# Full-width f32 products for the first two chunks of a fused attention and expert kernel, with the weights' high and low parts made later

## The chip, the cores and the metric

The kernel runs on one core of one Trainium2 chip. The metric is the device time of one execution in microseconds, the median of several runs. The core has a matmul engine (TensorE, PE in the profile), VectorE (DVE), ScalarE (ACT), GpSimd (POOL) and SyncE (SP), which here issues all transfers.

## What is computed

The input x has 8 sequences of 1024 tokens with 256 features, in float32. In short form:

```
qkv = x @ Wqkv + b;  q, k, v = split(qkv)
q, k = q - mean(q), k - mean(k)            # over features
q2 = q*q / (sum(q*q) + eps), scaled to unit length over features
k2 = k*k / (sum(k*k) + eps), scaled to unit length over the 1024 tokens
t2 = q2 @ (k2^T @ v) / sqrt(1024)          # no softmax: linear attention
x  = layernorm(x + (v + t2) @ Wln + bln)
sel    = sigmoid(x @ expert_sel^T)         # 16 experts
scores = relu(x @ keys[e])                 # 128 hidden features each
out    = sum over e of sel[e] * (scores @ values[e])
x  = layernorm(x + out)
```

## The kernel before, in words

Work goes by chunks of 512 tokens, 16 in all, two to a sequence. The projections of v and of the output are folded: `wy` stands for identity plus Wv @ Wln less its mean, and a 256x256 matrix M per sequence (`mh`, `ml`) carries k2^T x through Wv and Wln. For one chunk there are these steps: `tokens_x` loads x transposed (`xf`), `tokens_n` loads x token by token (`nf`); `u_k` projects keys (`kp`), squares and normalizes them (`k`) and multiplies with x (`ap`); `u_m` makes M from the sums of both chunks of a sequence (`mc`, `pm`, `mt`); `u_q` projects queries (`qp`), normalizes and transposes them (`qt`); `u_y` adds x @ wy (`ymx`) and q2 @ M (`ymq`) in `yp` and makes the gates; `u_pair` runs the experts, with `h` for the first product and `w` for the second; `u_end` closes with the second layernorm.

Almost every product is made from split operands. A float32 tile is cast on ScalarE (or VectorE) to the reduced format fp32r, its high part, and VectorE or GpSimd subtracts that from the original for the low part. `passes3` (line 52) then makes three fp32r matmuls out of each product:

```python
    return [(ah, bh), (ah, bl), (al, bh)]
```

So x has `xh`, `xl` and `nh`, `nl`; the weights have `wkh`, `wkl` (lines 460 to 475), `wqh`, `wql` (line 1309) and `wyh`, `wyl` (1306 to 1308); normalized keys have `k2h`, `k2l` (594 to 596), queries `q2h`, `q2l` (758 to 760) and M has `mh`, `ml` (688 to 699). A few products use unsplit float32 tiles, among them the centring of the weights (`wq_c`, `wl_c`, line 482) and the spreading of the first gates (`gsp`, line 844). In the chunks 0 and 1 the key and query biases enter as one more matmul with `rows` and `bhl`; from chunk 2 on VectorE adds them.

The order of the work is not written by hand. Each step is a task with an engine (or a choice of two), a cost, a key and the buffers that it reads and writes (`Work.add`, line 116). `Work.order` (line 202) plays the tasks through with these costs, engine by engine, and the program is issued in that order. Tasks that lead to the second expert products of the first three experts of chunk 0 are the goals' forebears: `sharpen` ranks them by the path still ahead of them, and they go first. All others go by their key. Buffers come from pools with a fixed number of slots (lines 41 to 45), and a task can be chosen only when its slots are free: `ld2` with three slots takes staged loads, `xh`, `xl`, `s4`, `ych` and `ycl` take parts, `t2` takes short-lived tiles. While goals are outstanding and TensorE has nothing that is ready, the planner puts in two small matmuls (`keep_warm`, line 433; tile `warm`), planned at 0.44 us:

```python
                        if e == "T" and self.idle and issued and first and now > 0.4:
                            fill = Task()
```

On the chip these fills are ordinary instructions in TensorE's queue. At the start of the program (lines 1213 to 1225) stand the loads of `sk` (the key weights), of x for the chunks 0 and 1, and of the other weights; then `u_k(0)`, `u_k(1)`, `u_q(0)`, `u_m(0)`, the first expert weights and `u_y(0)` (1251 to 1319), and `steady` (1321) brings in the later chunks while the experts of earlier ones run.

Of the kernel before, what the change touches and what calls it, by code (L numbers as in the profile page):

```python
# [15 lines left out]
P = 128  # L16
D = 256
# [13 lines left out]
FAST_FROM = 1  # L31
FAST_AT = 0.39
# [69 lines left out]
class Work:  # L102
# [13 lines left out]
    def add(self, eng, cost, key, fn, r=(), w=(), port=False, after=()):  # L116
# [6 lines left out]
        for many, writes in ((r, False), (w, True)):  # L123
            for x in many:
                b, part = x if isinstance(x, tuple) else (x, None)
                for other, opart, owrites in b.accesses:
                    if (writes or owrites) and meet(part, opart) and other is not t:
                        t.deps.add(other)
                b.accesses.append((t, part, writes))
                t.bufs[b] = None  # L130
        for d in t.deps:
            d.outs.append(t)
# [190 lines left out]
def attn_ffn_kernel(ctx, tc, x, xT, wqT, wk, wvT, wlnT, bcols, brows, selT, keys, values, outT):  # L323
# [55 lines left out]
    def high(key, h, b, n, r, w, free=True):  # L379

        if free:
            add("VS", {"V": c_dve(n, fast=True), "S": c_act(n, plain=True)}, key,
                {"V": lambda: V.tensor_copy(h(), b()), "S": lambda: S.copy(h(), b())}, r=r, w=w, port={"V": True, "S": False})
        else:
            add("S", c_act(n, plain=True), key, lambda: S.copy(h(), b()), r=r, w=w)
# [74 lines left out]
    def centered_rows(key, b, h, l):  # L460
# [8 lines left out]
        for k in range(2):  # L469
            add("VS", {"V": c_dve(D, fast=True, ptr=True), "S": c_act(D)}, key, {  # L470
                "V": lambda k=k: V.tensor_scalar(h[:, k], b[:, k], m[:, k : k + 1], None, ALU.add),
                "S": lambda k=k: S.activation(h[:, k], b[:, k], AF.Identity, bias=m[:, k : k + 1]),
            }, r=[b, m], w=[(h, k)], port={"V": True, "S": False})
            add("V", c_dve(D, ptr=True), key, lambda k=k: V.scalar_tensor_tensor(
                l[:, k], b[:, k], m[:, k : k + 1], f(h[:, k]), ALU.add, ALU.subtract), r=[b, m, (h, k)], w=[(l, k)], port=True)
# [15 lines left out]
    def high_low(key, t, h, l):  # L491
        add("S", c_act(CH, plain=True), key, lambda: S.copy(h.ap, halves(t.ap)), r=[t], w=[h])
        add("V", c_dve(CH), key, lambda: V.tensor_tensor(l.ap, halves(t.ap), f(h.ap), ALU.subtract), r=[t, h], w=[l])
# [5 lines left out]
    def in_first(c, tag, other):  # L499
        return other if c == 1 else tag  # L500

    def tokens_x(c, key):
        xh[c], xl[c] = h, l = [sbuf(t, [P, 2, CH], f"{t}{c}", FR) for t in ("xh", "xl")]
        if c == 0:
            b = sbuf("g3", [P, 2, CH], f"xf{c}")
            for i in range(2):
                w = slice(i * CH // 2, (i + 1) * CH // 2)
                add("D", 1.05, key, lambda w=w: nc.sync.dma_start(out=b[:, :, w], in_=xTv[:, :, w]), w=[(b, i)])
            for i in range(2):
                w = slice(i * CH // 2, (i + 1) * CH // 2)  # L510
                high(key + 1.2, lambda w=w: h[:, :, w], lambda w=w: b[:, :, w], CH, [(b, i)], [(h, i)])
                apply(key + 1.5, lambda w=w: l[:, :, w], lambda w=w: b[:, :, w], lambda w=w: f(h[:, :, w]), ALU.subtract,
                      CH, [(b, i), (h, i)], [(l, i)])
            return
        split(c, key, "xf", lambda s: xTv[:, s, c * CH : (c + 1) * CH], h, l, CH)

    def split(c, key, name, src, h, l, width):

        rows = h.shape[1]
        n = 1 if c < 2 else 2  # L520
        for i in range(n):
            s = slice(i * rows // n, (i + 1) * rows // n)
            part = None if n == 1 else i
            b = sbuf("g3" if c < 2 else "ld2", [P, rows // n, width], f"{name}{c}_{i}")
# [865 lines left out]
```

## Time and profile before

| | |
|---|---|
| median of 3 runs | 1022.59 us (1020.59 to 1023.46) |
| the profiled execution | 1020.05 us |
| its span, first to last instruction | 1018.3 us |
| mean granted clock of TensorE | 0.996 |
| busy: PE, DVE, ACT, POOL | 1008.1, 784.8, 667.1, 470.5 us |
| DMA | 99.52 MB, mean 98 GB/s |
| first projection starts (`kp`) | 9.18 us |
| first product of queries and M (`yp<-q2h,mh`) starts | 42.48 us |
| first second-layer product of an expert (`w`) starts | 63.96 us |

A line of the profile's timeline has the start, the time of the whole group, the engine, the line of the program, the operation and the tiles as out<-in, the shape and the number of instructions. Matmuls are pipelined: the duration of one is longer than the step to the next, so costs of TensorE are read from start to start. A float32 product that is not split leaves two records, a split one leaves three.

### The profile page before, as it was taken

How to read it: one execution, taken by the hardware profiler on the slowest of the kernel's cores; microseconds unless marked ns; L12 is line 12 of the kernel's file. 1: busy time of each engine (PE TensorE's matmuls, PEld its weight loads, DVE VectorE, ACT ScalarE, POOL GpSimd, SP SyncE). 2: the span in 40 equal slices, each digit the busy share in tenths (PEclk: the TensorE clock that was granted, in tenths of full speed). 3: DMA queues.
4: the chain of work that ended last, by engine and by line, in shares of the span. 5: the costliest groups of instructions: out<-in, count | busy, mean ns of one | idle time of the engine just before them, and what ended most of it. 6: DMA issues, size and time to landing. Idle time of an engine off the chain costs nothing.

```text
span 1018.3 us, 16317 instructions
## 1 busy us (share of the span) xinstructions
PE 1008.1 (99%) x5757; PEld 874.3 (86%) x5757; DVE 784.8 (77%) x1363; ACT 667.1 (66%) x1497; POOL 470.5 (46%) x424
## 2 busy tenths in 40 slices
PE   9999999999999999999999999999999999999996
PEld 9978879888898988889888888988889888888885
DVE  7889888687776887768787687867878687686775
ACT  7767566675676757766676676757666675665543
POOL 1001585546564464655536574454654536233430
PEclk9999999999999999999999999999999999999999
DMA  6144323233232323323223231323323222223131
GB/s 202 44 135 125 116 94 125 93 90 101 82 121 68 115 94 104 93 89 103 93 89 108 87 115 63 115 94 103 105 71 109 93 85 83 83 85 104 64 125 42
DMA packets 65298, 99.52 MB, mean 98 GB/s; under 512 B 6336, under 2 KB 24896, under 8 KB 65216
## 3 DMA queue, kind: packets, MB, share of 16 engines
q1 hardware_dynamic: 65216, 98.48, 30.1%
q8 instruction: 45, 0.74, 0.3%
q14 instruction: 37, 0.30, 0.1%
HBM read 89.54 MB, written 8.91 MB: 97 GB/s over the span
## 4 chain that ended last, share of the span: by engine, by line
PE 93%; DVE 3%; POOL 2%; ACT 1%; DMA 1%; issue 1%; POOLq 0%; DVEq 0%; ACTq 0%; SPq 0%
PE w L1121 32%; PE h L358 17%; PE hx L1074 11%; PE yp L358 8%; PE qp L358 4%; PE hy L1074 4%; PE kp L358 4%; PE ap L358 4%; PE warm L435 1%; PE qt L755 1%; PE sp L358 1%; PE pm L358 1%; DMA ksr<-keys 1%; PE mc L358 1%; DVE sl L1041 0%
## 5 line engine op out<-in xcount | busy, mean ns | idle before, releaser
L1121 PE MATMUL w<-sh,valh 128*128 128x512 f32 x504 | 158.4, 395 | 0.0
L1121 PE MATMUL w<-sh,vall 128*128 128x512 f32 x504 | 158.0, 394 | 0.0
L1121 PE MATMUL w<-sl,valh 128*128 128x512 f32 x504 | 157.7, 394 | 0.0
L1039 DVE SCALAR_TENSOR_TENSOR h<-h,selb 128x512 f32<-128x512 f32 x136 | 93.9, 692 | 31.0 <-PE h L358 27.8
L1121 PEld LDWEIGHTS w<-sh,vall 128*128 128x128 f32 x504 | 95.0, 188 | 22.1
L1121 PEld LDWEIGHTS w<-sl,valh 128*128 128x128 f32 x504 | 94.6, 188 | 22.4
L1040 ACT CAST sh<-h 128x512 fp32r<-128x512 f32 x136 | 73.6, 589 | 59.6 <-PE w L1121 55.5
L358 PE MATMUL h<-ych,keyh 128*128 128x512 f32 x272 | 109.7, 403 | 0.0
L358 PE MATMUL h<-ycl,keyh 128*128 128x512 f32 x272 | 107.5, 395 | 0.0
L358 PE MATMUL h<-ych,keyl 128*128 128x512 f32 x272 | 107.0, 393 | 0.0
L1041 DVE TENSOR_TENSOR sl<-h,sh 128x512 fp32r<-128x512 f32 x136 | 87.8, 683 | 23.1 <-ACT sh L1040 23.0
L1121 PEld LDWEIGHTS w<-sh,valh 128*128 128x128 f32 x504 | 86.2, 188 | 10.9
L389 POOL TENSOR_TENSOR k<-k,ks 128x512 f32<-128x512 f32 x25 | 30.9, 1257 | 101.9 <-DVE ks L566 101.9
L1093 DVE TENSOR_TENSOR hx<-hx,p 128x512 f32<-128x512 f32 x60 | 41.8, 696 | 29.8 <-ACT hy L1090 29.6
L1135 POOL TENSOR_TENSOR w<-w,ycl 128x512 f32<-128x512 f32 x30 | 38.2, 1296 | 55.5 <-DVE w L1132 55.5
L389 POOL TENSOR_TENSOR ysq<-ysq 128x512 f32<-128x512 f32 x15 | 20.1, 1338 | 91.1 <-ACT ysq L875 91.1
L358 PEld LDWEIGHTS h<-ych,keyl 128*128 128x128 f32 x272 | 51.1, 188 | 12.0
L358 PEld LDWEIGHTS h<-ycl,keyh 128*128 128x128 f32 x272 | 51.3, 189 | 10.5
L358 PEld LDWEIGHTS h<-ych,keyh 128*128 128x128 f32 x272 | 51.1, 188 | 10.7
L877 DVE SCALAR_TENSOR_TENSOR ycl<-yp,by,ych 128x512 fp32r<-128x512 f32 x32 | 24.0, 750 | 42.9 <-ACT ysq L875 42.9
L1090 ACT COPY hy<-hx 128x256 f32<-128x256 f32 x60 | 21.4, 357 | 46.9 <-PE hx L1074 45.4
L389 POOL TENSOR_TENSOR q<-q,qy 128x512 f32<-128x512 f32 x27 | 28.1, 1060 | 51.3 <-ACT sh L1040 43.7
(505 smaller groups left out, 3193.6 us busy)
## 6 DMA issues: line engine op xcount, KB each, us to landing
selb<-sel SPq DMA_DIRECT2D x253, 256.0 KB, 3.5
xf<-xT SPq DMA_DIRECT2D x30, 256.0 KB, 3.3
outT<-w SPq DMA_DIRECT2D x15, 512.0 KB, 3.0
nf<-x SPq DMA_DIRECT2D x28, 256.0 KB, 4.6
kst<-keys SPq DMA_DIRECT2D x6, 256.0 KB, 3.3
vst<-values SPq DMA_DIRECT2D x6, 256.0 KB, 3.7
nf<-x SPq DMA_DIRECT2D x2, 512.0 KB, 7.9
ksr<-keys SPq DMA_DIRECT2D x4, 256.0 KB, 3.5
```

What stands on the lines that cost most here:

```text
L358: T.matmul(out, w, r, start=first and i == 0, stop=last and i == len(terms) - 1)
L389: fns = {e: (lambda e=e: ENG[e].tensor_tensor(out(), a(), b(), op)) for e in engines}
L435: T.matmul(warm[:, :P], ones.ap, ones.ap, start=True, stop=True)
L877: add("V", c_dve(CH, ptr=True), k0 + 0.9, lambda t=t, jt=jt: V.scalar_tensor_tensor(yl[:, jt, :], t.ap, by[:, jt : jt + 1], f(yh[:, jt, :] ...
L1039: add("V", c_dve(CH), key + 0.1, lambda: V.scalar_tensor_tensor(at(t.ap), at(h.ap), 0.0, out(sel), ALU.max, ALU.mult), r=[h] + reads(sel), ...
L1040: add("S", c_act(CH, plain=True), key + 0.1, lambda: S.copy(out(a), at(t.ap)), r=[t], w=reads(a))
L1041: add("V", c_dve(CH), key + 0.1, lambda: V.tensor_tensor(out(b), at(t.ap), f(out(a)), ALU.subtract), r=[t] + reads(a), w=reads(b))
L1074: T.matmul(out(), wi, ri, start=first and i == 0, stop=True, skip_group_check=True)
L1090: add("S", c_act(n, plain=True), key + 0.07, lambda: S.copy(y1(), x1()), r=[x], w=[y])
L1093: add("V", c_dve(CH), key + 0.09, lambda: V.tensor_tensor(halves_(x.ap), halves_(x.ap), p5.ap.to_broadcast([P, 2, n]), ALU.add), r=[x, p5] ...
L1121: T.matmul(wps[c][v].ap, w[:, e % 4, v * P : (v + 1) * P], r[:, i], start=e == 0 and j == 0, stop=e == NE - 1 and j == 2)
L1135: add("G", c_pool(CH), key + 0.5, lambda v=v: G.tensor_tensor(w[:, v, :], w[:, v, :], f(ycl[c][:, v, :]), ALU.add), r=[(w, v), ycl[c]], w= ...
```

## The change

For chunk 0, the products of x with the key, query and output weights, of x with the keys, and of the queries with M are made from float32 tiles, without parts; for chunk 1 this holds for the products of x with the key weights and of x with the keys. The tiles for this are `x32`, `n32`, the normalized keys themselves, `q32` and `m32`; the loads write straight into slots of `xh`, `xl`, `s4` and `ych`. The parts of the three weights, and of chunk 1's x, which later products use, are made by tasks with late keys (`AT_SPLIT`, `late_split`). M is made in both forms for the first sequence. Queries of chunk 1 take their bias on VectorE.

In the planner a task can now hold buffers that it doesn't access, so that both slots of a pair are taken together. The cast of `nf` from chunk 2 on waits for the key casts of the chunk before and for the query transposes of two chunks before (`turns`), and casts of `high` are all on ScalarE.

```diff
+AT_SPLIT = -45
...
-    def add(self, eng, cost, key, fn, r=(), w=(), port=False, after=()):
+    def add(self, eng, cost, key, fn, r=(), w=(), port=False, after=(), hold=()):
...
+        for b in hold:
+            b.accesses.append((t, None, False))
+            t.bufs[b] = None
...
-    def high(key, h, b, n, r, w, free=True):
+    def high(key, h, b, n, r, w, after=(), hold=()):
+
+        return add("S", c_act(n, plain=True), key, lambda: S.copy(h(), b()), r=r, w=w, after=after, hold=hold)
...
-                "V": lambda k=k: V.tensor_scalar(h[:, k], b[:, k], m[:, k : k + 1], None, ALU.add),
-                "S": lambda k=k: S.activation(h[:, k], b[:, k], AF.Identity, bias=m[:, k : k + 1]),
-            }, r=[b, m], w=[(h, k)], port={"V": True, "S": False})
-            add("V", c_dve(D, ptr=True), key, lambda k=k: V.scalar_tensor_tensor(
-                l[:, k], b[:, k], m[:, k : k + 1], f(h[:, k]), ALU.add, ALU.subtract), r=[b, m, (h, k)], w=[(l, k)], port=True)
+                "V": lambda k=k: V.tensor_scalar(b[:, k], b[:, k], m[:, k : k + 1], None, ALU.add),
+                "S": lambda k=k: S.activation(b[:, k], b[:, k], AF.Identity, bias=m[:, k : k + 1]),
+            }, r=[m], w=[(b, k)], port={"V": True, "S": False})
+        high_low(AT_SPLIT, b, lambda: b.ap, h, l)
...
+    def late_split(c, key):
+        b = x32[c]
         xh[c], xl[c] = h, l = [sbuf(t, [P, 2, CH], f"{t}{c}", FR) for t in ("xh", "xl")]
+        add("S", c_act(2 * CH, plain=True), key, lambda: S.copy(h.ap, b.ap), r=[b], w=[h])
+        for i in range(2):
+            apply(key + 0.3, lambda i=i: l[:, i], lambda i=i: b[:, i], lambda i=i: f(h[:, i]), ALU.subtract, CH, [b, h], [(l, i)])
+
+    def split(c, key, name, src, h, l, width):
+
+        rows = h.shape[1]
+        in_turn = [turns[n] for n in (f"k{c - 1}", f"q{c - 2}") if n in turns]
...
+            high(key + 1.2, lambda s=s: h[:, s], lambda b=b: b.ap, CH, [b], [(h, i)], in_turn if name == "nf" else (), (l,))
...
+    def tokens_n(c, key):
+        if c < 2:
+            n32[c] = b = sbuf(("s4", "ych")[c], [P, 4, D], f"nf{c}")
+            add("D", 2.1, key, lambda: nc.sync.dma_start(out=b.ap, in_=x[c * CH : (c + 1) * CH, :].rearrange("(t p) d -> p t d", p=P)), w=[b])
             return
...
+    def project32(c, g, t, w, bias):
+
+        for j in range(2):
+            tk = slice((2 * g + j) * P, (2 * g + j + 1) * P)
+            mm_group(t[:, j * D : (j + 1) * D], [(x32[c][:, k, tk], w[:, k, :]) for k in range(2)] + [(rows[:, bias, :], bhl[:, 0])])
...
             for tt in range(4):
+                if c < 2:
+                    terms.append((n32[c][:, tt, dcol], q[:, tt, :]))
+                    continue
                 terms += passes3(nh[c][:, tt, dcol], nl[c][:, tt, dcol], h[:, tt, :], l[:, tt, :])
...
+            if c < 2 and i == 0:
+                two = sbuf("t2", [P, 2, D], f"k2s{c}")
...
+    m32 = sbuf("sl", [P, 2, D], "m32")
...
+        if b == 0:
+            def m32_():
+                for ct in range(2):
+                    S.activation(m32[:, ct, :], mt[:, ct * D : (ct + 1) * D], AF.Copy, scale=ky[:, ct : ct + 1])
...
+            if c == 0:
+                add("VS", {"V": c_dve(CH), "S": c_act(CH, plain=True)}, key + 7, {
+                    "V": lambda ct=ct, o=o: V.tensor_copy(q32[0][:, ct, :], o.ap), "S": lambda ct=ct, o=o: S.copy(q32[0][:, ct, :], o.ap),
+                }, r=[o], w=[(q32[0], ct)], port={"V": False, "S": False})
+                continue
...
+                if c == 0:
+                    terms.append((wy[:, k, cols], x32[c][:, k, :]))
+                    continue
                 terms += passes3(wyh[:, k, cols], wyl[:, k, cols], xh[c][:, k, :], xl[c][:, k, :])
...
+                if c == 0:
+                    terms.append((m32[:, k, cols], q32[0][:, k, :]))
+                    continue
                 terms += passes3(mh[b][:, k, cols], ml[b][:, k, cols], q2h[c][:, k, :], q2l[c][:, k, :])
...
-    wy = sbuf("t2", [P, 2, D], "wy")
+    wy = sbuf("sh", [P, 2, D], "wy")
...
-    add("S", c_act(CH, plain=True), -57, lambda: S.copy(wyh.ap, wy.ap), r=[wy], w=[wyh])
-    add("V", c_dve(CH), -56, lambda: V.tensor_tensor(wyl.ap, wy.ap, f(wyh.ap), ALU.subtract), r=[wy, wyh], w=[wyl], port=True)
-    high_low(-68, centered("wq", sq, -69, "att"), wqh, wql)
+    high_low(AT_SPLIT + 2, wy, lambda: wy.ap, wyh, wyl)
+    cq, wq = centered("wq", sq, -69, "att"), sbuf("sl", [P, 2, D], "wq")
+    add("S", c_act(CH, plain=True), -68, lambda: S.copy(wq.ap, halves(cq.ap)), r=[cq], w=[wq])
+    high_low(AT_SPLIT + 1, wq, lambda: wq.ap, wqh, wql)
...
+    late_split(1, AT_SPLIT + 3)
```

## The prediction

> **What bounds the kernel now.** I read the page first (busy shares, chain), then the TensorE timeline of the first 70 us, then windows around the holes in it, then VectorE and ScalarE in the same stretch.
>
> ```profile
> span 1018.3 us, 16317 instructions
> PE 1008.1 (99%) x5757; PEld 874.3 (86%) x5757; DVE 784.8 (77%) x1363; ACT 667.1 (66%) x1497; POOL 470.5 (46%) x424
> PE 93%; DVE 3%; POOL 2%; ACT 1%; DMA 1%; issue 1%; POOLq 0%; DVEq 0%; ACTq 0%; SPq 0%
> ```
>
> TensorE is busy throughout and carries 93% of the chain. "Busy" has modelled ends, so I checked starts against starts: from 70 us to the end matmuls follow each other at 0.118 us (256 columns) and 0.233 us (512 columns), with one hole of 1 us at 150. After the first stretch the time is therefore a sum of matmuls, and the result depends on two quantities only: matmul time added or removed, and TensorE time in the first 64 us that does nothing useful. The latter is shown by the filler matmuls `warm`:
>
> ```profile
> 1.06 8.37 PE L435 MATMUL warm<-ones 128*128 128x128 f32 x60 [1.06 <-POOL ones L423]
> 9.18 0.37 PE L358 MATMUL kp<-wkh,xh 128*128 128x256 f32 x1
> ...
> 15.87 1.89 PE L358 MATMUL wq_c<-ic,sq 128*128 128x256 f32 x8
> 17.60 1.89 PE L358 MATMUL wl_c<-ic,sl 128*128 128x256 f32 x8
> ...
> 33.16 0.61 PE L435 MATMUL warm<-ones 128*128 128x128 f32 x4
> ...
> 40.33 2.40 PE L435 MATMUL warm<-ones 128*128 128x128 f32 x20
> 42.48 0.48 PE L358 MATMUL yp<-q2h,mh 128*128 128x512 f32 x1
> ...
> 59.99 0.71 PE L435 MATMUL warm<-ones 128*128 128x128 f32 x4
> 60.63 1.12 PE L844 MATMUL gsp<-gs,pick 16*128 16x512 f32 x2
> 61.68 2.63 PE L435 MATMUL warm<-ones 128*128 128x128 f32 x12
> 63.96 1.20 PE L1121 MATMUL w<-sh,valh 128*128 128x512 f32 x2
> ```
>
> Read start to start, filler and waiting take 9.18 us before the first projection, 0.36 at 33, 2.15 at 40, 0.64 at 60 and 2.28 at 61.7: about 14.6 us. The other engines there:
>
> ```profile
> 9.18:40.33 31.15, 31.15 (x233) 29.83 (x232) 27.02 (x67) 25.14 (x67) 1.63 (x3) 1.00 0.32 102
> 40.33:42.48 2.15, 2.15 (x22) 2.15 (x21) 2.15 (x6) 1.44 (x3) 0.00 (x0) 1.00 0.00 0
> 62.05:65.47 3.42, 3.42 (x16) 3.09 (x15) 3.42 (x7) 1.90 (x4) 0.00 (x0) 0.50 0.67 203
> ```
>
> Columns: TensorE, weight loads, VectorE, ScalarE, GpSimd busy, then granted clock and DMA. VectorE is busy 27.0 of 31.2 us before the hole at 40 and all of it inside: what TensorE waits for there is queued on VectorE.
>
> **The change part by part.**
>
> *Matmul time.* A split product of 256 columns is three matmuls, 3 x 0.118 = 0.354 us. At full width it is one f32 matmul, two records: `wq_c` and `wl_c` are the same form, and four of them take 17.60 - 15.87 = 1.73 us, 0.4325 each. So +0.079 per product. Products: keys of chunks 0 and 1, 16; queries of chunk 0, 8; `ap` of both chunks, 16. 40 x 0.079 = +3.2 us. Of 512 columns there are 8 (`yp` of chunk 0): split 12 `yp` take 39.46 - 36.66 = 2.80 us, 0.70 per product. For full width the undisturbed 256-column row doubled gives 0.865; the two back-to-back `gsp` matmuls (58.08 to 59.99) give 0.955, but with waits in them and 16 rows. I take 0.865, +1.3 us (+2.0 at the other end). Together +4.5 us, all ahead of the end of `yp` of chunk 0. The queries of chunk 1 lose four bias matmuls, -0.47, and gain two VectorE additions of 0.69, not on the path.
>
> [...]
>
> *Start.* The first projection now needs centred `sk`, the bias row and `xf`, no splits. `sk_m` is ready at 4.57; two centring steps of 0.51 on ScalarE end near 5.6; the bias row's mean (to 5.07), high part and low part (0.34 + 0.48) end near 6; the first half of `xf` has landed when ScalarE takes it at 5.96. Data would allow about 6.2. But the fill count is fixed in the planned order: 15 fills of 8.12/15 = 0.541 us, planned at 0.44. With the planner's own costs on this path (transfer 4.4, both centrings, bias row about 5.5) I get 12 fills instead of 15: the start at 1.06 + 12 x 0.541 = 7.55, -1.6 us. Ends: 11 fills, -2.2, or 14, -0.5. The second half of `xf` (7.75) and chunk 1's (9.25) come in time.
>
> *VectorE and ScalarE before 42 us.* Removed at 0.60 us per step, start to start: `xl` 4, `nl` 4, `k2l` 4, `q2l` 2; the low parts of `wk`, `wq`, `wy` about 2.0; `k2h` 0.35. Some 10.8 us leave VectorE's critical work. Low parts of the three weights and of chunk 1's x (3.0 us) come back as late work, ScalarE loses some 6 us of casts, gets `m32` (0.9) and the late casts. Cost zero, covered by the room just made. Uncovered, the late split would hold back queries of chunk 1, which before ran at 33 and 45 us and whose transposes were at 66: 20 us of cover.
>
> *The holes at 33 and 40.* From 7.55 us the work needed before the `yp<-q` products is: keys 7.9, centring 3.5, `ap` 6.9, `pw` 1.7, queries 3.9, `pb` 2.6, `mc` 0.9, `pbb` 0.3, `pm` 1.4, `yp<-x` 3.5, transposes 0.9, together 33.5: ready at 41.0 if dense. Is the data there? Queries of chunk 0 can end by about 30 (keys, centrings, `ap` of chunk 0 before them). Their chain after that, read from the trace without its queueing: squares 1.0, inverse 0.4, second squares 2.6, Newton 1.7, scaling 1.3, transpose and copy 1.4, about 8.5 us: 38.5. The other branch (`ap` of chunk 1 to `asb`, `ah`, `al`, `pm`, `mt`, `m32`) needs 6. Both are below 41, so TensorE is what ends last and the fills at 33 and 40 go: -2.5. What was pulled forward into that stretch, one half of chunk 1's queries (33.52 to 35.25, 1.64), moves behind it: -1.6 there.
>
> End of `yp` for chunk 0, 45.34 before: -1.6 - 2.5 - 1.6 + 4.5 = -1.3 us, 44.0. (Adding up from the start instead, 41.0 + 3.5 = 44.5; the 0.5 is rounding of many short groups, and I keep the difference, in which it cancels.)
>
> *From there to the first `w` (18.6 us).* A chain through `tt`, `zt`, gates, transposes, `gsp`, `sh`, `sl`, in which nothing changes. The moved half of the queries (now 1.41) replaces fill at 60 to 64, cost zero; if it lands ahead of `tt` instead, +1.1, if the shorter queues on ScalarE let the gates through, about -1. I take zero. The clock: in 62.05:65.47 the granted clock was 0.50, and the first six `w` took 66.12 - 63.96 = 2.16 us where 1.40 is usual. [...] If it goes, -0.8.
>
> *Order and buffers.* `hold` and `after` make the cast of `nf` wait for the key casts of the chunk before and the query transposes two chunks before. In the steady part a cast at 361 would move behind transposes at 380; `ap` uses it at 416: 36 us of cover. Behind it wait its low part on GpSimd and, through the three `ld2` buffers, one `xf` transfer on SP's queue (364 before, cast at 388, used at 398). Cost zero; uncovered, about 1 us per chunk. The early transfers keep count and size and only change destination. SP already stands from 14.4 to 43.4 us for a fourth `ld2`; the late split of x must be done by then, or weight loads behind it slip, needed from about 70. The sums of k2 take a fresh `t2` buffer instead of working in place, `wy` leaves that pool: even.
>
> Sum on the profiled execution (1018.3 span, 1.75 around it, 1020.05): 1018.7. That execution lies 2.5 us below the median of 1022.59; the difference carries over to the median: 1022.59 - 1.3 = 1021.3.
>
> **Rivals.**
>
> *The gate stretch fills up too.* More early room on VectorE and ScalarE lets the gates run without queueing, and queries and h matmuls replace the fills at 60 and 61.7. `sl` was ready at 62.33 while `w` started at 63.96: 1.6 us, and 0.8 of slow clock. 1021.3 - 2.4 = 1018.9. For: fills overshoot their planned 0.44. Against: the transfers feeding other work are as late as before.
>
> *Slower: the query chain, not TensorE, ends last.* If the order puts the lengthened keys, `ap` of both chunks and centrings ahead of chunk 0's queries, these end at 7.55 + 7.9 + 3.5 + 6.9 + 1.7 + 3.9 = 31.5 instead of 27.75. If their chain keeps its 14.7 us (27.75 to 42.48), `yp<-q` starts at 46.2, +3.7, and is 0.65 longer; less 0.47 for the bias: +3.9, 1026.5. It decides once the chain from queries to `yp<-q` exceeds about 10 us. For: it did so by queueing before. Against: 10.8 us of that queue are gone.
>
> *Half of it.* The start moves, the hole at 40 stays and keeps its half of the queries: -1.6 + 4.5 - 0.5 = +2.4, 1025.0.
>
> **How the numbers follow.** About 0.3%, 3.1 us, is what a measurement of this kernel can tell from no change. Likeliest case, within 2 us of 1021.3: 0.42. Gate stretch filled as well: 0.28. Half of it: 0.12. Query chain: 0.18, in which I count other losses by order. Faster by over 0.3% needs below 1019.5: most of the second case and an edge of the first, 0.30. Slower needs over 1025.7: the query chain and an edge of the half case, 0.20. Same 0.50. The range leaves out about 0.1 on each side: 1017.6 to 1025.8.
>
> **What would show it.** The first `kp` near 7.5 with about 48 `warm` records before it; f32 `kp` products at 0.43; no `warm` between `kp` and `yp<-q`; end of chunk 0's `yp` near 44.0; first `w` near 62.7; no new holes after 70. I am wrong if full-width products cost 0.47 or more, if `warm` remains at 35 to 45, or if holes appear in the steady part.

## The result, and the profile after

The changed kernel takes 1031.12 us (median of 4 runs, 1030.46 to 1033.19), the kernel before in the same comparison 1022.91. The ratio is 1.0088, 95% interval 1.0066 to 1.0110: slower by about 9 us (8.2 between the medians), where 1021.3 us was predicted and 1025.8 was the end of the range. Runs of the kernel before fall into two groups, most from 1022.2 to 1023.8 us and some from 1018.9 to 1020.6 us; its profiled run, at 1020.05, is of the lower group, so the two profiled executions below are 10.5 us apart and not 8.2.

The head of the page of the changed kernel: span, busy time of each engine, and the chain that ended last by engine.

```profile
span 1028.8 us, 16164 instructions
PE 1015.3 (99%) x5693; PEld 876.7 (85%) x5693; DVE 774.8 (75%) x1353; ACT 663.2 (64%) x1495; POOL 472.7 (46%) x421
PE 72%; POOL 8%; ACT 7%; DVE 7%; issue 5%; DMA 0%; POOLq 0%; DVEq 0%; ACTq 0%
```

TensorE still shows 99% busy: short holes weigh little in 1028.8 us, and the modelled ends of matmuls cover part of them (of one of 0.89 us at 278, below, 0.73 us show as idle time). The chain tells more: TensorE's part in it fell from 93% to 72%, and GpSimd, ScalarE, VectorE and "issue" took the rest. Something in the steady part now ends later than TensorE.

TensorE's timeline of the first 70 us of the changed kernel, with the fills:

```profile
1.06 5.97 PE L436 MATMUL warm<-ones 128*128 128x128 f32 x36 [1.06 <-POOL ones L424]
...
7.11 1.50 PE L436 MATMUL warm<-ones 128*128 128x128 f32 x12
8.44 1.03 PE L363 MATMUL kp<-sk,xf 128*128 128x256 f32 x4
9.12 0.47 PE L363 MATMUL kp<-bhl,rows 128*128 128x256 f32 x1
9.43 1.02 PE L363 MATMUL kp<-sk,xf 128*128 128x256 f32 x4
...
16.29 1.89 PE L363 MATMUL wq_c<-ic,sq 128*128 128x256 f32 x8
18.01 1.89 PE L363 MATMUL ap<-k,nf 128*128 128x256 f32 x8
...
40.91 1.50 PE L436 MATMUL warm<-ones 128*128 128x128 f32 x12
42.25 3.60 PE L363 MATMUL yp<-q,m 128*128 128x512 f32 x8
...
47.10 0.61 PE L436 MATMUL warm<-ones 128*128 128x128 f32 x4
...
58.57 1.06 PE L436 MATMUL warm<-ones 128*128 128x128 f32 x8
59.60 1.98 PE L870 MATMUL gsp<-gs,pick 16*128 16x512 f32 x4
61.51 0.71 PE L436 MATMUL warm<-ones 128*128 128x128 f32 x4
62.15 1.61 PE L870 MATMUL gsp<-gs,pick 16*128 16x512 f32 x2
63.69 2.93 PE L436 MATMUL warm<-ones 128*128 128x128 f32 x12
66.84 1.05 PE L1157 MATMUL w<-sh,valh 128*128 128x512 f32 x2
```

There are 48 `warm` records ahead of `kp`, the 12 fills that were predicted, but `kp` starts at 8.44 and not at 7.55. The first product of queries and M starts at 42.25, 0.2 us earlier than before. The fill at 33 is gone, the one at 40.91 is still there, and new ones stand at 47.10 and 58.57. The first `w` comes at 66.84, 2.9 us later than before.

Three windows of the changed kernel (busy time and count of TensorE, weight loads, VectorE, ScalarE and GpSimd, then granted clock, DMA share and GB/s):

```profile
8.44:40.91 32.47, 32.47 (x169) 27.71 (x167) 21.80 (x58) 20.55 (x58) 0.68 (x3) 1.00 0.30 94
40.91:42.25 1.34, 1.34 (x15) 1.34 (x13) 1.32 (x3) 1.34 (x4) 0.00 (x0) 1.00 0.00 0
62.65:69.48 6.83, 6.83 (x22) 5.12 (x21) 6.11 (x15) 3.48 (x9) 0.00 (x0) 0.50 0.49 154
```

VectorE has the promised room (21.8 of 32.5 us), and yet TensorE waits at 40.91. In this pair of profiles the half-clock stretch has doubled, from 3.41 to 6.83 us. What TensorE waits for at 40.91 is the second copy of `q` on ScalarE. TensorE's steps ahead of it, and ScalarE's:

```profile
38.32 0.60 PE L776 MATMUL qt<-ident,q 128*128 128x128 f32 x4
38.75 1.88 PE L363 MATMUL yp<-xf,wy 128*128 128x512 f32 x4
40.47 0.60 PE L776 MATMUL qt<-ident,q 128*128 128x128 f32 x4
```

```profile
38.95 0.58 ACT L781 COPY q<-qt 128x512 f32<-128x512 f32 x1 [1.64 <-PE qt L776]
...
40.24 0.90 ACT L702 ACTIVATE mh<-mt,ky 128x256 fp32r<-128x256 f32 x2
41.04 0.60 ACT L386 CAST xh<-xf 128x512 fp32r<-128x512 f32 x1
41.55 0.58 ACT L781 COPY q<-qt 128x512 f32<-128x512 f32 x1
```

The casts of `mh` and `xh`, which chunk 0 doesn't need, stand ahead of the second copy. But the first copy started 0.63 us after its transposes did; at that distance the second would have started at 41.10, so the casts delay it by only 0.45 us. The rest of the 1.34 us is the way from the transposes to the copy and on to `yp`, with nothing left for TensorE to do beside it: the second transposes stand behind half of the products `yp<-xf,wy`, though the first ones already had all of the normalized queries that both need (VectorE ended them at 37.25).

Behind 70 us the two traces keep drifting apart. The hole at 278, first on TensorE, then on ScalarE:

```profile
276.76 0.28 PE L1110 MATMUL hx<-ych,keyl 128*128 128x256 f32 x1
...
277.58 0.39 PE L363 MATMUL sp<-ycl,ewt 128*128 128x512 f32 x1
...
278.70 0.38 PE L1110 MATMUL hx<-th,ksh 128*128 128x256 f32 x1 [0.73 <-ACT p L1120]
```

```profile
276.75 1.25 ACT L797 COPY yv4s<-ysq 64x512 f32<-64x512 f32 x2
...
277.90 0.36 ACT L1119 COPY hy<-hx 128x256 f32<-128x256 f32 x1
...
278.28 0.37 ACT L1120 COPY p<-hx 128x256 f32<-128x256 f32 x1
```

`hx` is complete at about 276.9, but its copies `hy` and `p` stand in ScalarE's queue behind two `yv4s` copies of 1.25 us. The next `hx` needs the bank that `p` empties. From the start of the last `sp` it comes after 1.12 us where 0.23 is usual: a hole of 0.89. Others stand at 400.64, 523.66, 646.69 and 769.80 (0.89 to 0.90), and six of 0.25 to 0.29 between `hx` and `wv` at 214, 337, 460, 583, 706 and 829. One set per sequence, 5 x 0.89 + 1.6 = 6.0 us. Before has only one hole of over 0.2 us between 70 and 1000 us, of 1.05 at 150.

A sum over matmuls from start to start puts the profiled executions side by side. "Start" is fill time ahead of `kp`, "fills" those after it, "clock" half of the half-speed time that lies on matmuls other than fills, "rest" all other time, holes included. With the 1.06 us ahead of the first matmul they give the start of the last one.

| us | start | fills | clock | rest | last matmul |
|---|---|---|---|---|---|
| before | 8.12 | 5.44 | 0.75 | 994.34 | 1009.71 |
| after | 7.06 | 6.03 | 2.12 | 1004.23 | 1020.51 |
| difference | -1.06 | +0.59 | +1.37 | +9.89 | +10.80 |

Of the 9.9 us, 4.0 are matmul work as predicted (+4.5 - 0.47); the remainder is about the size of those holes. The experiments test that, and ask where the promised fills and the clock went. The theory was: **A**, the wait of the `nf` casts changes the planned order, and so makes the holes; **B**, the longer matmuls cost their own time; **C**, late work on ScalarE and VectorE, started just ahead of a gate step, lengthens the stretch to the first `w`. The rival to A was that the early part (late splits, other buffers) shifts the later phases.

### The profile page after: what moved, and what is told of

It is laid out like the page before. It is cut to its first block, busy times and chain, and to the rows that moved or that the text cites. A ratio compares the mean times of both kernels' runs of the same rounds, so it can differ in the third digit from the quotient of the medians.

```text
span 1028.8 us, 16164 instructions
## 1 busy us (share of the span) xinstructions
PE 1015.3 (99%) x5693; PEld 876.7 (85%) x5693; DVE 774.8 (75%) x1353; ACT 663.2 (64%) x1495; POOL 472.7 (46%) x421
## 4 chain that ended last, share of the span: by engine, by line
PE 72%; POOL 8%; ACT 7%; DVE 7%; issue 5%; DMA 0%; POOLq 0%; DVEq 0%; ACTq 0%
PE w L1157 25%; PE h L363 10%; PE hx L1110 9%; PE qp L363 4%; PE kp L363 4%; PE ap L363 4%; PE hy L1110 4%; PE yp L363 4%; POOL nl L390 1%; POOL xl L390 1%; PE warm L436 1%; POOL w L1171 1%; PE pm L363 1%; POOL q L390 1%; ACT qj L745 1%
## 5 line engine op out<-in xcount | busy, mean ns | idle before, releaser
L363 PEld LDWEIGHTS h<-ych,keyl 128*128 128x128 f32 x272 | 51.1, 188 | 12.1
L913 DVE SCALAR_TENSOR_TENSOR ycl<-yp,by,ych 128x512 fp32r<-128x512 f32 x32 | 24.0, 750 | 46.8 <-ACT ysq L911 46.8
L1129 DVE TENSOR_TENSOR hx<-hx,p 128x512 f32<-128x512 f32 x60 | 41.5, 691 | 23.1 <-ACT hy L1126 21.8
L390 POOL TENSOR_TENSOR kss<-kss 128x512 f32<-128x512 f32 (+1 forms) x20 | 25.1, 1255 | 67.5 <-ACT kss L602 67.5
```

Source lines behind the costliest of these rows:

```text
L363: T.matmul(out, w, r, start=first and i == 0, stop=last and i == len(terms) - 1)
L390: fns = {e: (lambda e=e: ENG[e].tensor_tensor(out(), a(), b(), op)) for e in engines}
L913: add("V", c_dve(CH, ptr=True), k0 + 0.9, lambda t=t, jt=jt: V.scalar_tensor_tensor(yl[:, jt, :], t.ap, by[:, jt : jt + 1], f(yh[:, jt, :] ...
L1129: add("V", c_dve(CH), key + 0.09, lambda: V.tensor_tensor(halves_(x.ap), halves_(x.ap), p5.ap.to_broadcast([P, 2, n]), ALU.add), r=[x, p5] ...
```

## The experiments

### 1 and 2: the wait of the `nf` casts

The changed kernel, with the wait limited to chunks 2 and 3 (without any wait the kernel's planner finds no order):

```diff
-            high(..., in_turn if name == "nf" else (), (l,))
+            high(..., in_turn if name == "nf" and c <= 3 else (), (l,))
```

> The changed kernel, but the cast of nf waits for earlier key casts and query transposes only up to chunk 3; later chunks cast as soon as buffers are free. Theory A (that wait reorders ScalarE's queue in the steady part, and TensorE then waits about 1.2 us per sequence, five times): the holes of 0.9 us after sp disappear and the time falls by about 6 us from 1031.1, to about 1025. Theory B (the steady holes follow from the later and different start, or from the shared hold of the two part buffers, not from the wait): holes stay, about 1031.

And the other way round, the kernel before with that wait and nothing else of the change:

```diff
+        in_turn = [turns[t] for t in (f"k{c - 1}", f"q{c - 2}") if t in turns]
...
-            high(..., c < 2)
+            high(..., c < 2, in_turn if name == "nf" and c > 1 else ())
```

> The kernel before, with nothing added but the wait of the nf casts for the key casts of the chunk before and the query transposes two chunks before. Theory A: the steady holes of about 0.9 us after sp appear in a kernel whose first 60 us are the old ones, and the time rises by about 6 us, to about 1029. Theory B: unchanged, about 1023.

Measured: the first 1027.06 us (1025.25 to 1027.49), ratio to before 1.0038 [1.0023, 1.0053]; the second 1029.96 us (1026.77 to 1030.26), 1.0060 [1.0043, 1.0076]. Before, in that comparison, took 1022.78.

The same place in the second kernel, which has no full-width product:

```profile
275.18 0.40 PE L358 MATMUL sp<-ycl,ewt 128*128 128x512 f32 x1
276.30 0.39 PE L1075 MATMUL hx<-th,ksh 128*128 128x256 f32 x1 [0.71 <-ACT p L1085]
```

The hole is there, 0.89 us, and again at 398, 522, 646 and 769. In the first kernel, ScalarE at that place:

```profile
277.71 1.25 ACT L797 COPY yv4s<-ysq 64x512 f32<-64x512 f32 x2 [0.56 <-POOL ysq L390]
279.62 0.36 ACT L1119 COPY hy<-hx 128x256 f32<-128x256 f32 x1 [0.66 <-PE hx L1110]
279.99 0.37 ACT L1120 COPY p<-hx 128x256 f32<-128x256 f32 x1
```

Here the `yv4s` copies run 1.7 us ahead of `sp` instead of 0.13, ScalarE is idle for 0.66 us when `hx` arrives, and the holes are gone. "Rest" falls to 998.20, 3.86 above before: the matmul work alone. In the second it is 1002.10, 7.8 above before, with no matmul added. A is shown in both directions, and the rival falls. The wait needn't delay TensorE itself: it moves other steps. Counted back from the end of the traces, some 755 of ScalarE's 1256 instructions after 150 us are at another place than before in the second kernel and 765 in the changed one, but only 10 in the first. That the first kernel gained only 4 of the 6 us is mostly the clock: in the profiles its half-speed stretches cost 4.59 us of work, 2.5 more than in the changed kernel, and its start took 0.9 more, since the clock was full at 6.54 us instead of 4.63; its fills took 0.75 less.

### 3 and 4: late work that gives way

To test C, a rule in the planner: while goals are outstanding, a late task isn't started on an engine if a task on the way to a goal becomes ready there before it would end. First in experiment 1, then (ScalarE and VectorE alone) in the kernel before.

```diff
+                        if first and t.tail is None and e in "SVT" and any(
+                                o.tail is not None and now + 1e-9 < w < now + t.cost[e] - 0.0 for _, _, o, w in ready[e]):
+                            continue
```

> As the first of these kernels, and the planner doesn't start a late task on VectorE, ScalarE or TensorE, while the first experts' goals are outstanding, if a goal task would become ready on that engine before it ends. Theory C (late work, which can't be interrupted, stands in front of the gate chain of chunk 0 and makes its first w late): first w near 63 instead of 66.8, five fewer fills, and 2 to 4 us less than the first kernel, about 1022. Theory D (only the added matmul time counts after the steady holes are gone): within 0.5 us of the first kernel.

> The kernel before with the same giving way on VectorE and ScalarE. Theory C: the first w comes about 2 us earlier (62 instead of 64), but only one fill goes, since the work that filled the gap is the same; the time falls by 0.4 to 1 us, about 1022. Theory D: no change, 1023.

Measured: 1026.93 us (1025.39 to 1027.83), 1.0039 [1.0024, 1.0054]; and 1023.98 (1018.37 to 1024.55, 20 runs), 1.0002 [0.9989, 1.0015]. The first `w` does come at 62.54 where the changed kernel has it at 66.84 and experiment 1 at 69.62 (half clock ahead of it took 4.2 us in experiment 1 and 1.7 here), and fills after the start fall to 3.92 us. But what gave way is missed later: holes of 1.30 (in `ap`), 0.24, 0.62, 0.66 and 1.10 between 109 and 150 us, where experiment 1 has one of 0.60, put "rest" 3.4 us above that. C is right on the stretch and wrong on the total.

The fourth told something else. Its 20 runs lie between 1018.4 and 1020.6 (six of them) or between 1021.9 and 1024.6 (14), and its profiled run, at 1018.51, had no half-speed stretch ahead of the last chunk. The kernel before shows two groups too: in the comparison of experiment 5, 16 runs from 1018.9 to 1020.5 and 19 from 1022.2 to 1023.2. The mean granted clock that was recorded with each run goes with the groups: over all experiments, 40 runs of before up to 1020.5 us had 0.996 to 0.998, and 66 from 1022.2 us on had 0.994 or 0.995. In the fourth, the five runs up to 1018.9 had 0.997, the others 0.992 to 0.995. So the groups differ by time at half clock; one more stretch of 3.41 us at 0.50 lowers the mean over a span of 1018 us by 0.0017.

### 5, 6 and 7: the thin columns

Experiment 1 had half clock right behind `tt` (1 column) and `zt` (48 columns) and again on the first `w`:

```profile
50.90:57.70 6.80, 6.80 (x23) 5.74 (x23) 5.56 (x17) 4.66 (x13) 0.00 (x0) 0.50 0.37 116
68.00:71.40 3.40, 3.40 (x13) 2.92 (x13) 3.14 (x9) 2.01 (x6) 0.00 (x0) 0.50 0.61 233
```

TensorE is busy in both, and from 30 us on no step ahead of them is more than 0.4 us longer than usual. A new theory, **H**: the half-speed stretches follow those stretches in which TensorE is busy but its matmuls move few columns (`tt` 1, `zt` 48) or few rows (`gsp` 16). The first two groups were widened to 128 columns, with the extra ones unread, in the kernel before (5), in experiment 4 (6) and in experiment 1 (7).

```diff
-            mm_group(zt[:, 64 * j : 64 * j + 48], [(u[:, k, tk], ewt[:, k, 0:48]) ...])
+            mm_group(zt[:, P * j : P * (j + 1)], [(u[:, k, tk], ewt[:, k, :]) ...])
...
-            mm_group(tt[:, j : j + 1], [(sq[:, k, tk], ones[:, 0:1]) for k in range(2)])
+            mm_group(tt[:, P * j : P * (j + 1)], [(sq[:, k, tk], ones.ap) for k in range(2)])
```

> Edit: the kernel before, in which the two thin matmul groups of the gate stage, the token sums tt (one output column each) and the gate scores zt (48 columns each), write 128 columns each, with the columns beyond the needed ones left unread. A matmul of either group lasts about 0.11 us in the profile at 1, at 48 and at 128 columns, so TensorE's own work should be the same. Theory H (the half-speed stretches of the first 75 us follow the stretches in which TensorE is busy but moves few columns): the stretch of 3.41 us at half clock no longer starts behind tt and zt, the profile shows the clock at full from 4 us to the end, and the times gather near 1018 to 1019.5 instead of 1022.8, ratio about 0.996 to 0.997. Rival (the half-speed stretch comes from the thin gsp matmuls with 16 rows and the fills near 60 us, or from something outside the kernel): the stretch stays, times as before, 1022 to 1023.

> Edit: both the wide tt and zt columns and the planner's rule of the fourth experiment (late work on ScalarE and VectorE gives way to the gate stage) in the kernel before. Theory H: about 1018.5 in nearly all runs, since the fourth experiment's profiled run without a half-speed stretch took that; ratio about 0.996. Rival: the times stay split as in the fourth experiment, 1018.4 to 1020.6 in a third of the runs and 1022 to 1024.5 in the rest, with a median near 1023.5.

> Edit: the first experiment (the change, with the wait of the nf casts limited to chunks 2 and 3) with the wide tt and zt columns. It lost 4.6 us of work to two half-speed stretches, and has 3.9 us more matmul work than the kernel before. Theory H: both stretches go or shrink to the one near 68 us, time 1022 to 1024.5, ratio against the kernel before about 1.000. Rival (half-speed stretches are not of these matmuls): 1026.5 to 1027.5 as in the first experiment, ratio 1.004.

Measured, against 1022.34 of before: 1020.02 us (1019.27 to 1020.64, 13 runs), 0.9987 [0.9978, 0.9996]; 1020.51 (1018.13 to 1021.95, 22 runs), 0.9990 [0.9980, 0.9999]; 1024.80 (1024.16 to 1025.44), 1.0041 [1.0026, 1.0055]. So 5 beats before, though by less than H expected, and its 13 runs lie in one group (granted clock 0.996 to 0.998). 6 still has two, 8 runs to 1018.7 (all 0.997) and 14 from 1020.4 (0.994 to 0.997). 7 came out between the two expectations, nearer to H: of two half-speed stretches the second is left. The stretch from 46.8 to 58 and the rest in experiment 7:

```profile
46.80:58.00 11.20, 11.20 (x81) 10.34 (x80) 8.99 (x24) 8.58 (x21) 0.00 (x0) 1.00 0.31 95
64.80:68.10 3.30, 3.30 (x13) 2.98 (x13) 3.30 (x8) 2.34 (x7) 0.00 (x0) 0.50 0.42 142
```

H holds for the columns (1.00 from 46.8 to 58, where experiment 1 had 0.50 for 6.8 us); the edit leaves the order of all instructions as it was. The stretch behind `gsp`, which contracts over 16 rows, is untouched (0.50 from 64.8 to 68.1).

### 8: half of the full-width contraction

Is the time ahead of `yp` TensorE's own? In experiment 7, half of every full-width product is left out, in the same order:

```diff
-            mm_group(..., [(x32[c][:, k, tk], w[:, k, :]) for k in range(2)] + [...])
+            mm_group(..., [(x32[c][:, k, tk], w[:, k, :]) for k in range(1)] + [...])
```

and likewise in `ap` (two of four terms) and in both products of `yp`.

> Edit: the seventh experiment (the change, wait limited to chunks 2 and 3, wide gate columns), in which every full-width float32 product of chunks 0 and 1 leaves out the second half of its contraction; the planner still counts the whole, so the order of all instructions is the same. Left out: 20 steps of 256 columns at 0.4325 us and 4 of 512 columns at 0.865 us, 12.1 us of TensorE work. Theory T (TensorE's own work is what the end of yp and all behind it wait for, so a microsecond more of matmul work is a microsecond more of time): yp ends about 12 us earlier, the time is 1012 to 1015, and few holes open. Rival (the chains over ScalarE and VectorE end last before yp, and matmul time beside them is partly hidden): holes of several microseconds open in the first 45 us, the time falls by less than 8 us, to 1017 or more.

Measured: 1022.36 us (1021.67 to 1023.19), 1.0015 [1.0003, 1.0027] of before, which took 1020.30 in this comparison, with 12 of its 21 runs in the lower group. Theory T was wrong here and the rival right, though the time, 2.4 us less than in experiment 7, says it more sharply than the rival did: of 12.1 us taken away only 3.9 arrive at the end of `yp` and 2.9 at the last matmul. The largest part, 4.4 us, is lost in a hole, and some 3 us in a half-speed stretch from 27.2 to 34.0 us, which starts inside that hole. TensorE in that kernel:

```profile
22.88 1.03 PE L363 MATMUL ap<-k,nf 128*128 128x256 f32 x4
28.13 3.78 PE L363 MATMUL pw<-wlc,svT 128*128 128x256 f32 x8 [4.22 <-ACT wlc L1309]
```

ScalarE in the same stretch waits for VectorE:

```profile
24.42 0.91 ACT L995 ACTIVATE valh<-vst,vst_m 128x256 fp32r<-128x256 f32 x2 [2.43 <-DVE vst_m L992]
...
27.51 0.57 ACT L1309 COPY wlc<-wl_c 128x512 f32<-128x512 f32 x1
```

`wlc` stands in ScalarE's queue behind `valh`, whose mean `vst_m` waits for VectorE, and that is busy without a gap from 18.8 to 24.2 us, over half of it with the sums of `k2` and `kss`. So in this order matmul time counts one for one only as long as this queue ends earlier: of the time removed two thirds are lost by the end of `yp`. The order was planned for the whole products, so another order could give more.

### 9: one part alone

Of the change only the keys of chunk 0 at full width, in experiment 5:

```diff
+            if c == 0:
+                add("T", c_mm(D, 4, full=True) + c_mm(D, 2), key + g, lambda g=g, t=t: project32(c, g, t, sk, 1),
+                    r=[(x32[c], g), sk, rows, bhl], w=[t])
+                squares(key + g + 0.7, q, g, s, t)
+                continue
```

with `wk` centred in place, split later (at key -180, where the change has -45), and the wait for chunks 2 and 3.

> Edit: the fifth experiment (the kernel before with wide gate columns), and of the change one part alone: only the keys of chunk 0 are multiplied at full width, with wk centred in place and split for chunk 1 later, and the casts of chunks 2 and 3 wait as in the first experiment (without that the planner finds no order). Matmul work +0.6 us by the durations of the trace (8 steps of 0.4325 us for 24 of 0.118 us). Theory (the start is worth about 1 us, since wk and x need not be split before the first kp, but what is won at the start is spent again behind yp on fills, as in the changed kernel): first kp 0.6 to 1.2 us earlier than in the fifth experiment, yp ends 0 to 1 us earlier, the first w comes no earlier, time 1020 to 1022, ratio to the kernel before 0.999 to 1.001. Rival (the start's gain lasts): 1018.5 to 1019.5, ratio about 0.997.

Measured: 1024.07 us (1023.56 to 1024.66), 1.0030 [1.0019, 1.0041] of the same 1020.30, slower than either theory had it. Beside the profile of experiment 5, the start gained 1.2 us (first `kp` at 9.64, in experiment 5 at 10.52, and `pbb` now ahead of it; about 0.3 of it because the clock was full at 6.19 us and not at 6.85), matmul work and holes cost 0.5, the clock 0.5, but the fills after the start rose from 4.52 to 8.88 us:

```profile
33.82 2.03 PE L436 MATMUL warm<-ones 128*128 128x128 f32 x16
40.73 2.40 PE L436 MATMUL warm<-ones 128*128 128x128 f32 x20
58.69 1.50 PE L436 MATMUL warm<-ones 128*128 128x128 f32 x12
62.03 0.71 PE L436 MATMUL warm<-ones 128*128 128x128 f32 x4
63.72 2.51 PE L436 MATMUL warm<-ones 128*128 128x128 f32 x12
66.46 1.06 PE L436 MATMUL warm<-ones 128*128 128x128 f32 x4
```

Here a small step at the start costs more in the order behind it than it saves. Which of its three edits brings the fills is not shown.

### 10, 11 and 12: the thin rows too

`gsp` over 128 rows, 112 of them zeros, in experiments 5, 6 and 7:

```diff
-        gs = sbuf("t2", [P, CH], "gs")
+        gs = sbuf("sl", [P, CH], "gs")
+        add("G", 0.9, key + 0.9, lambda: G.memset(gs.ap, 0.0), w=[gs])
...
-            ... T.matmul(o.ap, pick[:NE, e, :], gs[:NE], start=True, stop=True) ...
+            ... T.matmul(o.ap, pick[:, e, :], gs.ap, start=True, stop=True) ...
```

> Edit: the fifth experiment (the kernel before with wide tt and zt columns), in which the three gsp products, which contract over 16 rows only, contract over 128 rows, 112 of them zeros. A full-width product of 512 columns lasts 0.86 us on 128 rows in the trace, and a gsp of 16 rows about as long, so TensorE's work stays the same; GpSimd gets one clearing of 128x512. Theory H (few rows count as little activity just as few columns do): the half-speed stretch near 62 us that is left in some runs goes too, the range of the times narrows below the 1.4 us of the fifth experiment, and the median is 1019.0 to 1020.0. Rival (the fills or the mixture in front of the first w set the clock, or nothing is left to be won in the fifth experiment): 1019.3 to 1020.7 as there.

> Edit: the sixth experiment (wide tt and zt columns, late work gives way) with the gsp products over 128 rows as in the tenth. The sixth had 8 runs at 1018.1 to 1018.7 and 14 at 1020.4 to 1022.0. Theory H (the upper group are runs in which a half-speed stretch of 3.41 us falls on the gsp products and the w behind them): all runs at 1018.1 to 1019.0, ratio about 0.997. Rival (the upper group has another cause): two groups as before, with the median above 1020.

> Edit: the first experiment (the change, wait limited to chunks 2 and 3) with wide tt and zt columns and gsp over 128 rows, as the tenth has them for the kernel before. What is left of the difference between the two kernels when neither loses time to the clock and the steady order is the same. Theory T: 3.9 us of matmul work, about 1 us of fills in front of the first w, less 1 us at the start: 1018.4 + 3.9 = 1022.3, range 1021.5 to 1023.5. Rival (the lost half-speed time was part of the change's own cost in all runs and the rest is free): 1019 to 1020.5.

Measured: 1018.40 us (1017.86 to 1019.37, 5 runs), 0.9962 [0.9949, 0.9974]; 1019.17 (1018.66 to 1020.24, 6 runs), 0.9969 [0.9957, 0.9981]; 1021.85 (1020.79 to 1022.40, 12 runs), 0.9995 [0.9985, 1.0004]. The tenth beats both kernels: 4.4 us below before, and 0.6 under the expected range. The eleventh has one group only, its range a little above the expected one. The granted clock was 0.998 in all runs of 10 and 12 and 0.997 or 0.998 in those of 11; in experiment 5 it was 0.996 in four of 13 runs, in 7 it was 0.994 to 0.997. So less time was at half clock with 128 rows, as with 128 columns; by what measure the clock is granted no run shows.

But the clock is not all that 10 gains on 5. Neither profile has a half-speed stretch ahead of the last chunk, and yet the last matmul comes 1.50 us earlier: 0.94 of this is the start, where the clock was full at 4.86 us and not at 6.85, and 0.66 lies between the first `gsp` and the first `w`. In experiment 5 and in 10:

```profile
59.43 1.98 PE L844 MATMUL gsp<-gs,pick 16*128 16x512 f32 x4
61.34 0.71 PE L435 MATMUL warm<-ones 128*128 128x128 f32 x4
```

```profile
58.38 1.88 PE L845 MATMUL gsp<-gs,pick 128*128 128x512 f32 x4
60.10 0.61 PE L435 MATMUL warm<-ones 128*128 128x128 f32 x4
```

From start to start the two products take 1.91 us with 16 rows and 1.72 with 128, and the fill behind them 0.64 and 0.44. So "about as long" in the expectation of 10 was not exact. 10 has the order of 5 on TensorE, VectorE and ScalarE; 12 has another order than 7 from 62 us on, with two fills more.

Experiment 12 in the stretches that were at half clock:

```profile
46.80:58.00 11.20, 11.20 (x79) 10.30 (x78) 8.99 (x25) 8.66 (x22) 0.00 (x0) 1.00 0.27 84
58.00:72.00 14.00, 14.00 (x78) 10.93 (x77) 11.79 (x29) 10.05 (x28) 0.00 (x0) 1.00 0.44 135
```

Full clock from 6 us to the last chunk. With clock and steady order put aside on both sides, the change itself is the difference of 12 and 10:

| us | start | fills | clock | rest | last matmul |
|---|---|---|---|---|---|
| 10: before, wide | 8.52 | 4.22 | 0.00 | 994.24 | 1008.03 |
| 12: change, wait to chunk 3, wide | 7.71 | 5.36 | 0.00 | 997.48 | 1011.60 |
| difference | -0.81 | +1.14 | 0.00 | +3.24 | +3.57 |

3.6 us in the profiled executions, 3.45 in the medians: the matmul work is paid nearly in full, and what the start gives goes back as fills. The start of 12 would show some 0.5 us more gain if its clock had been full at 4.86 us, as in 10, and not at 6.00.

## Why the prediction was wrong

Two steps failed, by similar amounts. "Order and buffers: cost zero" became 6.0 us of holes in the steady part. And the fills, which were to shrink by some 5.5 us (1.6 at the start, 2.5 at 33 and 40, 1.4 at 60 to 64 by the moved half of the queries), shrank by 0.5 in the profiles (-1.06 and +0.59). The added matmul work was right, so nothing was left to pay for it. Of the prediction's own signs of being wrong two came true: `warm` remains between 35 and 45, and holes appear in the steady part.

- **Matmul time: right.** A `kp` group of two full-width products and bias steps in 0.98 to 0.99 us, `ap` takes 1.73 for four, and experiment 1 has 3.86 us more in "rest" where 4.0 was the sum. No run shows the 0.47 that the prediction names as its limit for a full-width product; they show 0.4325 per 256 columns.
- **Start: right in kind, half in size.** 12 fills, as worked out. But `pbb` (0.33 us) moved in front of `kp`, and the fills cost 7.06/12 = 0.59 instead of 0.54 each, with the clock full only from 4.63 us (4.03 before). -0.74 for the first `kp` instead of -1.6. About 0.3 us of the difference is chance, since that moment differs between runs with one and the same order too (6.85 us in experiment 5, 4.86 in 10).
- **Holes at 33 and 40: wrong.** The sum took the work as dense up to `yp<-q` and asked only whether the data for it would be ready. It counted the transposes and their copy into a chain that would be ready at 38.5; in the order that was issued the second transposes come last on TensorE, at 40.47, their copy on ScalarE follows with nothing beside it, and other casts stand ahead of it. Fills there fell by 1.17 us, not by 2.5. The moved half of the queries did leave the stretch (1.73 us from start to start, where the prediction has 1.64). `yp` ends at 42.25 + 8 x 0.4325 = 45.7, not at 44.0. The rival "half of it" was right that the hole at 40 stays (1.34 of 2.15 us), and wrong that it keeps its half of the queries.
- **From `yp` to the first `w`: wrong.** "I take zero" became +2.5: fills in it rose from 2.92 to 4.68 us, and half speed covered 4.2 us ahead of the first `w`, 1.9 before. The moved half of the queries was to replace fill; instead the order moved half of chunk 2's keys behind the first `w`.
- **Clock: right that it stays, wrong that it stays the same.** The sum takes nothing off for the half-speed stretch behind `gsp` and fills, and it stayed (0.50 from 62.65 to 69.48). That it belongs to the thin matmuls the experiments bear out: with wider ones the granted clock was 1.00 from 48 to 72 us in the profiles of 5, 10 and 12. Half speed that begins in a long hole shows only in experiment 8 (at 27.2 us, in a hole of 4.2 us from 23.9). But one profile was taken for a constant. In the profiles half speed falls at different places and costs 0 to 4.6 us; it was 1.4 us more in this pair. Between the medians it should count for little: the typical run of before had a granted clock of 0.994 or 0.995 too, as the changed kernel's four had.
- **Order and buffers: the step with the largest cost.** "Cost zero" rested on 36 us of cover for the cast that waits. The cast had it: it ran at 382.6, and its `ap` at 425.6. The cost lies in the other steps, which the planner put in another order because of the wait: 6.0 us of holes in the steady part. The price "about 1 us per chunk" was near in kind (1.2 us per sequence), but it was kept as a case of lost cover, and in the chances it stood only among the "other losses by order" within the 0.18 of the query chain. Without these holes (experiment 1) the time is still 1027.06, above the range: the matmul work adds 3.9 us to it, and half speed cost 4.59 us in its profile.
- **The premise that time is a sum of matmuls** holds upwards only. In experiment 8 a hole of 4.4 us, ended by ScalarE and VectorE, opened as soon as matmuls were taken away, so even saved matmuls would have given little in that order.

## What to carry to other kernels

Where a planner writes the order, a new constraint has no cover of its own: compare the order of all steps in one steady period, and multiply the smallest new hole by the number of periods before calling it free. When an engine at 99% gets work, add it in full (of 4.0 us of matmul work, experiment 1 has 3.86 more in "rest"); when it loses work, look for the queue that ends next (of 12.1 us taken away in experiment 8, 2.9 arrive at the last matmul). And compare the times and granted clocks of all runs, not only one profile, where a stretch at low clock is near.

## What the runs showed of the hardware

In these runs half clock also came where matmuls follow each other without a gap. `tt` with 1 column and `zt` with 48 step at 0.11 us (before), as they do with 128 (experiment 5); behind them, and behind `gsp` over 16 rows, the granted clock went to 0.50 for 3.4 or 6.8 us, at places that differ from run to run. With 128 columns and 128 rows (experiments 10, 11 and 12) each profiled run kept it at 1.00 up to the last chunk (mean 0.998). The rows are told apart from the columns by experiments 7 and 12 (clock loss 0.92 and 0.00, granted clock 0.994 to 0.997 in all runs of one and 0.998 in all of the other). The higher group of the times of before is the runs with the lower granted clock; that its additional stretch lies on `tt` and `zt` is argued from experiment 5, where the group is gone, and from experiment 2, which has the order of before on TensorE up to 144 us and shows 6.83 us at half clock from 50.04 on, in `zt`. No profile of before itself shows it.

The clock becomes full at 4.03 us in the profile of before, at 4.63 in that of the changed kernel, and at 6.54, 6.85, 6.19, 4.86 and 6.00 in experiments 1, 5, 9, 10 and 12. Until then the same `warm` matmul steps at 0.21 us, and at 0.11 after it (before: 0.213 and 0.112), so this time alone moves the start by up to 1.4 us, half of 6.85 - 4.03. Half speed starts at 62.06 us in the profile of before (for 3.41 us), at 62.65 in that of the changed kernel (6.83) and at 50.04 in experiment 2 (6.83); it holds throughout the windows 50.90:57.70 and 68.00:71.40 of experiment 1 and 64.80:68.10 of experiment 7. What sets the place, and with it the group of times that a run of before falls into, no run shows.

A float32 matmul of 256 columns, unsplit, costs 1.22 of three split ones (0.4325 us in `wq_c` of before, against 3 x 0.118 = 0.354).

Where matmuls over 16 rows and over 128 follow each other, the steps at the change are about 0.1 us longer (in the changed kernel the first step of `gsp` takes 0.53 us and the next two 0.43, the first of the fill behind it 0.21 and the next 0.11); inside `gsp` a step takes 0.43 us with either (16 rows there, 128 in experiment 10).
